# Decoder layer in fp32 split matmuls: other slots and engines for splits and a rounding piece in five of 32 attention units

## The chip, the core and the metric

The kernel runs on one core of one Trainium2 chip. The metric is the device time of one execution in microseconds (us). Most executions of this kernel agree within 0.3%. The core's engines run side by side and wait for each other through semaphores: TensorE (PE) multiplies, VectorE (DVE), ScalarE (ACT) and GpSimd (POOL) work on tiles, SyncE (SP) starts the transfers. PE also has a row of its own for loading weights (PEld).

## The reference

One decoder layer over x of 8 x 256 x 512, with a context of 8 x 256 x 512: rotary causal self-attention with 16 heads of 128, whose weights are a signed exponential; masked cross-attention over the context with 16 heads of 32; a feed-forward part of width 2048 with weights rounded to -1, 0 and 1 and activations rounded to 8 bits. Each of the three is added to x and normalized.

```python
def _L0_attn_ref(...):
    q = jnp.einsum('bpd,hde->bphe', resid_pre, W_Q) + b_Q
    ...
    q = _apply_rotary(q, cos, sin)
    k = _apply_rotary(k, cos, sin)
    scores = jnp.einsum('bqhd,bkhd->bhqk', q, k) / ATTN_SCALE
    ...
    scores = jnp.where(causal[None, None], scores, jnp.zeros((), dtype=scores.dtype))
    max_v = jnp.max(jnp.abs(scores), axis=-1, keepdims=True)
    sgn = jnp.sign(scores)
    attn_w = sgn * jnp.exp(sgn * scores - max_v)
    attn = attn_w / (jnp.sum(jnp.abs(attn_w), axis=-1, keepdims=True) + 1e-06)
    z = jnp.einsum('bkhd,bhqk->bqhd', v, attn)
    out = jnp.einsum('bqhd,hdm->bqm', z, W_O) + b_O
...
def weight_quant(w):
    scale = 1.0 / jnp.clip(jnp.mean(jnp.abs(w)), EPS, None)
    return jnp.clip(jnp.round(w * scale), -1.0, 1.0) / scale
...
x = _layernorm(x + _L0_attn_ref(x, ...), axis=-1)
x = _layernorm(x + _L0_xattn_ref(x, ctx_2048, mask_BxS2_ik0, ...), axis=-1)
x = _layernorm(x + _L0_ffn_ref(x, ...), axis=-1)
```

## The kernel before

**Split products.** A float32 operand is held as two parts, hi (a cast to the matmul type) and lo (the operand minus hi). Each product is three matmuls: hi x hi (L146), hi x lo (L147), lo x hi (L148). So every operand first needs a split: a cast and a subtraction over 128 x 1024 elements. `split` (L155) casts on DVE (L156) and subtracts on a given engine (L157). `half_split` (L181) does one of the two: part 1 is the subtraction (L183), part 0 the cast, on ACT (L185) or on DVE (L187). `x_half` applies it to one half of an x tile, `load_x` loads and splits both halves of one, `load_w` loads and splits a weight.

**Self-attention in 32 units.** A unit is a pair of heads times a pair of batches; the first four units share one head pair. Each takes about 28.1 us. Unit i computes its projections while the attention of unit i-1 runs, and the output projection of unit i-2 its end. A string of letters (`SCHED`, one for unit 0, one for all others) gives the program order, and `emit` walks it. Q is a projection, w and u its evictions on ACT (L308) and DVE (rcos, L314); r and R the rotation on POOL (L318, L324, L326); H and L the split of the rotated tile (L335 on ACT, L342, with the copy L341 of early keys on DVE); V, v, f the values. Of the unit before: s scores (L370, and mm3), a their eviction on ACT (L379, L380), S the causal select on POOL (L385), m the maximum on DVE (L391, L392), x the exponential on ACT (L400), n and N the sum and the normalization on DVE (snorm, L405 and L413, result e), t the transposes on PE (L420), c and k their split, z the product with the values, y and l its split (ACT L447, DVE), o the output projection, d its sum into acc (DVE, L465). The first digit after a letter is the batch half, the second the head.

**Slots.** B0, BA, BV, BW, BX, BY, XA, XB, X0, X1, G0 and G1 in the string are slots that `background(ui)` fills with work for later: loads of the next x and of weights, their splits, and the rounding of feed-forward weights. Units 1 to 3 read x from the input and split it in two halves; later units read the split tile back from DRAM. `wq_round` rounds one chunk of 128 x 1024 in three DVE steps (L219 scale and limit, L221 limit and add, L224 subtract), and then stores it; units 16 to 30 round one chunk each, and unit 17 rounds two (`ROUND`).

**Last unit.** Unit 31 loads the first half of the context (`cr`) and splits it, and loads and splits the second half of the first cross-attention weights (`wk1`); after it follow two value weights (`wv`), the values' bias (in a buffer of the tag aw, which has two), the second context tile (`ctx1`, subtractions on POOL, L157), the projections of keys and values for cross-attention (L146 to L148 into ppj, evicted by L634 and L638), with the attention of the last unit in between them (`tail`).

**Order.** `in_order` fixes the program order on ACT, DVE, POOL and SP up to the end of unit 31, for unit 0 on PE as well. PE's order in units 1 to 31, and every engine's in the stretch after unit 31, are set by the framework's scheduler. Buffers are few (`BUFS`: 5 for weights w, 2 for x tiles xt, 3 for raw loads, 2 for aw; in PSUM, 3 for projections and 1 for scores). The rest of the kernel (cross-attention, feed-forward) goes by a planned order that the change leaves alone.

Of the kernel before, what the change touches and what calls it, by code (L numbers as in the profile page):

```python
# [11 lines left out]
F32R = mybir.dt.float32r  # L12
# [47 lines left out]
SCHED = {  # L60
    "first": (
        "Q000 Q100 Q001 WK w00 u00 Q101 w10 u10 WV r00 R00 BA r10 Q010 Q011 w01 u01 H00 L00 Q110 R10 Q111 w11 u11 H10 L10 r01 V0 v0 V1 v1 "
        "X0 V2 v2 V3 v3 X1 R01 H01 L01 r11 R11 H11 L11 f0 f2 BW"
    ),
    "unit": (
        "B0 BP Q000 s00 Q001 a00 s01 a01 w00 Q010 u00 S0 BA s10 r00 Q011 m0 o00- o01- a10 w01 d00- R00 X0 s11 r01 H00 x0 a11 XA "
        "o10- Q100 S1 Q101 u01 o11- w10 d01- L00 n0 m1 R01 XB r10 H01 N0 u10 R10 L01 x1 Q110 n1 Q111 w11 t00 d11- "
        "t01 V0 v0 BV H10 c01 k01 u11 r11 V1 v1 c00 V2 k00 N1 X1 f0 z00 G0 z01 y0 t10 t11 c10 R11 c11 V3 H11 l0 k10 k11 BX "
        "L10 L11 BY v2 z10 z11 G1 y1 d10- v3 BW f2 l1"
    ),  # L70
# [8 lines left out]
def decoder_kernel(ctx: ExitStack, tc: tile.TileContext, a, out):  # L79
    nc = tc.nc  # L80
# [27 lines left out]
    def T(tag, shape, dt=F32, name=None):  # L108
        return (keep if tag in ("w", "xt") else sb).tile(shape, dt, name=name or tag, tag=tag, bufs=BUFS.get(tag, 1))
# [45 lines left out]
    def split(hi, lo, raw, eng):  # L155
        nc.vector.tensor_copy(hi, raw)  # L156
        eng.tensor_tensor(lo, raw, f32(hi), ALU.subtract)  # L157

    def split_w(raw, tag="w"):
        w = T(tag, [128, 2, 1024], F32R)  # L160
        split(w[:, 0], w[:, 1], raw, nc.vector)
        return w
# [13 lines left out]
    def x_half(t, raw, i, part, eng):  # L176
        tf = t.rearrange("p h k c -> p h (k c)")
        cs = slice(1024 * i, 1024 * i + 1024)
        half_split(tf[:, 0, cs], tf[:, 1, cs], raw, part, eng)

    def half_split(hi, lo, raw, part, eng):  # L181
        if part:
            eng.tensor_tensor(lo, raw, f32(hi), ALU.subtract)  # L183
        elif eng is nc.scalar:
            eng.copy(hi, raw)  # L185
        else:
            eng.tensor_copy(hi, raw)  # L187
# [13 lines left out]
    def wchunk(wi, c):  # L201
        return raw_load(a[f"w{wi + 1}T"][:, 1024 * c : 1024 * c + 1024])

    def wq_abs(raw, wi, c):
        nc.scalar.activation(raw, raw, AF.Abs, accum_out=absum[:, wi, c : c + 1])
# [11 lines left out]
    def wq_round(raw, wi, c, step):  # L217
        if step == 0:
            nc.vector.tensor_scalar(raw, raw, wscale[:, 2 + wi : 3 + wi], 1.0, ALU.mult, ALU.min)  # L219
        elif step == 1:  # L220
            nc.vector.tensor_scalar(raw, raw, -1.0, MAGIC, ALU.max, ALU.add)  # L221
        else:
            q = T("bc", [128, 1024], (BF16, F16)[wi], name="wqt")
            nc.vector.tensor_scalar(q, raw, -MAGIC, None, ALU.add)  # L224
            nc.sync.dma_start(wq_s[wi][:, 1024 * c : 1024 * c + 1024], q)
# [25 lines left out]
    hw, kv0 = {}, {}  # L251
# [233 lines left out]
    units = [Unit(hp, bp) for hp in range(NHP) for bp in range(NBP)]  # L485

    def run(fs):
        for f in fs:
            f()
# [22 lines left out]
    A0, ABS, late = 6, (4, 5, 6, 8, 9, 10, 12, 13), {}  # L512
    ROUND = {16: [0], 17: [1, 2], **{i: [i - 15] for i in range(18, 31)}}

    def background(ui):
        u = units[ui]
        ex = {k: [] for k in ("B0", "BA", "BV", "BW", "BX", "BY", "XA", "XB", "X0", "X1", "G0", "G1", "BP", "WK", "WV")}
        if ui == 0:
            ex["WK"].append(lambda: load_hp(0, "wK", first["wK"]))
            ex["WV"].append(lambda: load_hp(0, "wV", first["wV"]))  # L520
        nx = units[ui + 1] if ui + 1 < len(units) else None
        if nx is not None and nx.hp == 0:
            if ui < 2:
                ex["BA"].append(nx.xload)
            for i, k in enumerate(("X0", "X1") if ui < 2 else ("B0",)):
                ex[k].append(lambda i=i: nx.xsplit(i))
            if ui == 2:
                ex["XA"].append(lambda: x_half(nx.xt, nx.raws[1], 1, 0, nc.scalar))
                ex["XB"].append(lambda: x_half(nx.xt, nx.raws[1], 1, 1, nc.gpsimd))
        elif nx is not None:  # L530
            ex["BA"].append(nx.load)
        if ui == 1:
            ex["BV"].append(units[3].xload)
        if u.hp == 0:
            ex["BA" if ui else "X1"].append(lambda: init_acc(u.bp))
            ex["BA" if ui else "X1"].append(lambda: nc.sync.dma_start(f32(xs[u.bp][:]), f32(u.xt[:])))
        if "wv" in late:
            ex["B0"].append(lambda raw=late.pop("wv"): load_hp(u.hp, "wV", raw["w"]))
        for n, hp, k1 in ([("wO", u.hp, "BW")], [], [("wQ", u.hp + 1, "BW")], [("wK", u.hp + 1, ""), ("wV", u.hp + 1, "")])[u.bp]:
            if (ui or n == "wO") and hp < NHP:  # L540
                raws = {}
                ex["BV" if n == "wV" else "BA"].append(lambda n=n, hp=hp, raws=raws: raws.update(w=raw_load(a[n][hp])))
                if n == "wV":
                    late["wv"] = raws
                elif n == "wK":
                    def hi(raws=raws, hp=hp):
                        w = hw.setdefault(hp, {})["wK"] = T("w", [128, 2, 1024], F32R)
                        half_split(w[:, 0], w[:, 1], raws["w"], 0, nc.scalar)

                    def lo(raws=raws, hp=hp):  # L550
                        w = hw[hp]["wK"]
                        half_split(w[:, 0], w[:, 1], raws["w"], 1, nc.vector)

                    ex["G0"].append(hi)
                    ex["BX"].append(lo)
                else:
                    ex[k1].append(lambda n=n, hp=hp, raws=raws: load_hp(hp, n, raws["w"]))
        if ui in ABS:
            for j in range(2):
                i, rr = 2 * ABS.index(ui) + j, {}  # L560
                ex["BA"].append(lambda i=i, rr=rr: rr.update(w=wchunk(i // 8, i % 8)))
                ex[f"G{j}"].append(lambda i=i, rr=rr: wq_abs(rr["w"], i // 8, i % 8))
        for n, ci in enumerate(ROUND.get(ui, ())):
            cr = {}
            ex["BA"].append(lambda cr=cr, ci=ci: cr.update(w=wchunk(ci // 8, ci % 8)))
            for step, k in enumerate((("G0", "G1", "BW"), ("X0", "X1", "BX"))[n]):
                ex[k].append(lambda step=step, cr=cr, ci=ci: wq_round(cr["w"], ci // 8, ci % 8, step))
        if ui == 1:
            ex["BA"].append(lambda: bo.update(t=bcast("bc", "bO")))
        if ui == len(units) - 2:  # L570
            ex["BA"].append(lambda: kv0.update(wk0r=raw_load(a["wkx"][:, 0:1024])))
            ex["BW"].append(lambda: kv0.update(wk0=split_w(kv0["wk0r"])))
        if ui == len(units) - 1:
            ex["BA"].append(lambda: kv0.update(cr=x_raws(a["ctxT"][0])))

            def ctx_split(i):
                if i == 0:
                    kv0["ctx"] = T("xt", [128, 2, 4, 512], F32R)
                x_split(kv0["ctx"], kv0["cr"][i], i, (nc.vector, nc.gpsimd)[i])

            ex["X0"].append(lambda: ctx_split(0))
            for k, part, e in (("BX", 0, nc.vector), ("BY", 1, nc.gpsimd)):
                ex[k].append(lambda part=part, e=e: x_half(kv0["ctx"], kv0["cr"][1], 1, part, e))
            ex["X0"].append(lambda: kv0.update(wk1r=raw_load(a["wkx"][:, 1024:2048])))
            ex["BW"].append(lambda: kv0.update(wk1=split_w(kv0["wk1r"])))
        if ui == 4:
            ex["BA"].append(setup_late)
        if ui == 5:
            ex["G0"].append(setup_late2)
        if ui in (A0 + 8, A0 + 9):  # L590
            ex["G0"] += [lambda wi=wi: (wq_tot, wq_mean)[ui - A0 - 8](wi) for wi in range(2)]
        if A0 + 2 <= ui < A0 + 18:
            ex["BP"].append(lambda: add_bo(ui - A0 - 2))
        return ex
# [17 lines left out]
    for ui, u in enumerate(units):  # L612
        spec = SCHED["unit" if ui else "first"]
        if ui == 1:
            spec = spec.replace(" V0 v0", "").replace(" t00", " V0 v0 t00")
        emit(spec, u, units[ui - 1] if ui > 0 else None, units[ui - 2] if ui > 1 else None, background(ui))
        if ui == 0:
            in_order(["PE", "Activation", "DVE", "Pool", "SP"])
# [32 lines left out]
    H, steps, tiles, unit, last, readers = {}, [], {}, [None], {}, {}  # L651
# [747 lines left out]
```

## Time and profile before

| what | value |
|---|---|
| median of 3 runs | 1399.37 us |
| lowest, highest | 1399.22, 1401.14 us |
| profiled execution: its time | 1400.85 us |
| profiled execution: its span, first to last instruction | 1399.1 us |
| mean granted TensorE clock | 0.986 |
| unit 0's first matmuls to unit 31's end | 0 to some 915 us |
| DMA traffic | 170.13 MB, mean 122 GB/s |

Times inside a profile count from the first instruction. Busy time of PE contains the time in which it works at a lower granted clock, so a stretch can be full and yet slow. The span in 40 slices of 35 us (each digit the busy share in tenths) shows where the engines are less than full:

```profile
PE   8999999999999999999999999999999999988896
...
PEclk9999999999999999999999999999999999999998
```

### The profile page before, as it was taken

To read this page: it belongs to the slowest core of one execution; us is meant where nothing else is said; L and a number is where in the kernel's file an instruction comes from. 1 tells how busy PE (TensorE), PEld (TensorE's weight loads), DVE (VectorE), ACT (ScalarE), POOL (GpSimd) and SP (SyncE) were. 2 spreads that over 40 slices of the span, in tenths; PEclk is the share of its full clock that TensorE was granted. 3 is DMA by queue.
4 is the path that set the end of the run, shared out by engine and by line. 5 is a ranking of instruction groups with operands and counts; after the bars stand their busy time and mean duration, and the time that the engine had idled before them with its cause. 6 is when DMAs were issued, how large, how long until landed. Compare 5 with 4: busy or idle time off the path is not lost.

```text
span 1399.1 us, 23786 instructions
## 1 busy us (share of the span) xinstructions
PE 1355.8 (97%) x8576; PEld 1085.2 (78%) x8576; DVE 1100.3 (79%) x2040; ACT 876.1 (63%) x1944; POOL 785.7 (56%) x987
## 2 busy tenths in 40 slices
PE   8999999999999999999999999999999999988896
PEld 7789888998899878998899888878667667543342
DVE  7787777778768868887877877968767877798997
ACT  3766776777666656666665666533644445576994
POOL 5666556666665756766665656525033324376763
PEclk9999999999999999999999999999999999999998
DMA  8542342234223234223422442226324424214553
GB/s 280 206 184 107 134 156 106 91 144 161 91 75 121 90 128 162 105 83 126 187 84 98 132 167 98 76 90 197 113 58 126 135 72 140 91 31 91 114 113 98
DMA packets 84903, 170.13 MB, mean 122 GB/s; under 512 B 47025, under 2 KB 57009, under 8 KB 79921
## 3 DMA queue, kind: packets, MB, share of 16 engines
q1 hardware_dynamic: 84784, 168.61, 35.8%
q8 instruction: 68, 1.11, 0.3%
q14 instruction: 51, 0.41, 0.1%
HBM read 130.31 MB, written 27.79 MB: 113 GB/s over the span
## 4 chain that ended last, share of the span: by engine, by line
PE 75%; DVE 14%; issue 3%; POOL 3%; DMA 2%; ACT 2%; SPq 0%; POOLq 0%; DVEq 0%; ACTq 0%
PE ppj L146 12%; PE ppj L147 12%; PE ppj L148 12%; PE pz L146 3%; PE pz L148 3%; PE pz L147 3%; PE pwt L420 3%; PE sc L854 2%; PE den L885 2%; PE psc L370 2%; PE av L869 2%; PE pz L443 2%; PE ppo L146 2%; PE ppo L147 2%; PE ppo L148 2%
## 5 line engine op out<-in xcount | busy, mean ns | idle before, releaser
L318 POOL TENSOR_TENSOR sw<-sw,stab 128x512 f32<-128x512 f32 x128 | 170.5, 1332 | 98.7 <-ACT sw L309 98.2
L146 PE MATMUL ppj<-xt,w 128*128 128x512 f32 x528 | 209.7, 398 | 1.0 <-DVE w L156 0.7
L147 PE MATMUL ppj<-xt,w 128*128 128x512 f32 x528 | 207.2, 392 | 1.1 <-DVE xt L157 1.0
L148 PE MATMUL ppj<-xt,w 128*128 128x512 f32 x528 | 206.7, 392 | 0.0
L146 PE MATMUL ppj<-w,xt 128*128 128x256 f32 (+1 forms) x528 | 157.9, 299 | 1.7 <-DVE u L314 1.7
L148 PE MATMUL ppj<-w,xt 128*128 128x256 f32 (+1 forms) x528 | 152.2, 288 | 0.0
L147 PE MATMUL ppj<-w,xt 128*128 128x256 f32 (+1 forms) x528 | 152.1, 288 | 0.0
L342 POOL TENSOR_TENSOR rh<-u,rh 128x512 fp32r<-128x512 f32 x64 | 97.4, 1522 | 97.1 <-PE ppj L148 85.2
L314 DVE SCALAR_TENSOR_TENSOR u<-ppj,bqk,ctab 128x512 f32<-128x512 f32 x128 | 95.5, 746 | 71.6 <-ACT sw L309 71.1
L308 ACT ACTIVATE sw<-ppj,bqk 64x512 f32<-64x512 f32 x128 | 87.7, 685 | 93.3 <-PE ppj L148 88.4
L326 POOL TENSOR_TENSOR u<-u,sw 128x256 f32<-128x256 f32 (+1 forms) x128 | 131.8, 1029 | 6.4 <-DVE u L314 6.2
L413 DVE SCALAR_TENSOR_TENSOR e<-aw,rd,sg 128x128 f32<-128x128 f32 (+1 forms) x256 | 131.0, 569 | 0.1
L385 POOL TENSOR_SCALAR_AFFINE_SELECT aw<-aw 128x256 f32<-128x256 f32 x128 | 59.2, 486 | 104.5 <-ACT aw L379 104.5
L148 PEld LDWEIGHTS ppj<-xt,w 128*128 128x128 f32 x528 | 99.6, 189 | 21.7 <-DVE w L157 0.3
L400 ACT ACTIVATE aw<-aw,nm 128x256 f32<-128x256 f32 (+1 forms) x256 | 113.3, 444 | 4.9 <-DVE nm L391 2.6
L447 ACT CAST z<-pz 128x512 fp32r<-128x512 f32 x64 | 37.6, 587 | 122.8 <-PE pz L443 122.8
L146 PEld LDWEIGHTS ppj<-xt,w 128*128 128x128 f32 x528 | 99.7, 189 | 18.2 <-DVE w L156 1.0
L147 PEld LDWEIGHTS ppj<-xt,w 128*128 128x128 f32 x528 | 99.6, 189 | 18.3 <-DVE xt L157 1.8
L146 PEld LDWEIGHTS ppj<-w,xt 128*128 128x128 f32 x528 | 102.1, 193 | 3.2 <-issue 1.6
L147 PEld LDWEIGHTS ppj<-w,xt 128*128 128x128 f32 x528 | 102.2, 194 | 0.7
L148 PEld LDWEIGHTS ppj<-w,xt 128*128 128x128 f32 x528 | 101.9, 193 | 0.7
L379 ACT ACTIVATE aw<-psc 128x384 f32<-128x384 f32 x128 | 62.2, 486 | 61.7 <-PE psc L148 59.3
(284 smaller groups left out, 3950.0 us busy)
## 6 DMA issues: line engine op xcount, KB each, us to landing
xt<-xs SPq DMA_DIRECT2D x28, 2048.0 KB, 8.1
xs<-xt SPq DMA_DIRECT2D x4, 2048.0 KB, 13.0
raw<-w1T SPq DMA_DIRECT2D x16, 512.0 KB, 9.6
raw<-w2T SPq DMA_DIRECT2D x16, 512.0 KB, 9.7
raw<-wO SPq DMA_DIRECT2D x8, 512.0 KB, 9.0
acc<-xn SPq DMA_DIRECT2D x4, 1024.0 KB, 8.4
wq<-wqt SPq DMA_DIRECT2D x16, 256.0 KB, 2.4
kx<-ks SPq DMA_DIRECT2D x8, 512.0 KB, 5.0
```

The costliest lines, as they stand in the source:

```text
L146: nc.tensor.matmul(ps, lh, rh, start=first, stop=False)
L147: nc.tensor.matmul(ps, lh, rl, start=False, stop=False)
L148: nc.tensor.matmul(ps, ll, rh, start=False, stop=last)
L308: nc.scalar.activation(sw[0:64], ps[64:128], AF.Identity, bias=bias[64:128])
L314: nc.vector.scalar_tensor_tensor(v3(u), v3(self.ps.pop((h, i))), self.bias(h, i), ctab.to_broadcast([128, 2, 256]), ALU.add, ALU.mult)
L318: nc.gpsimd.tensor_tensor(v3(sw), v3(sw), stab.to_broadcast([128, 2, 256]), ALU.mult)
L326: nc.gpsimd.tensor_tensor(u, u, sw, ALU.add)
L342: (nc.gpsimd if i else nc.vector).tensor_tensor(lo, u if i else u[:, :, 128:256], f32(hi), ALU.subtract)
L379: nc.scalar.activation(aw[:, h], sc3, AF.Abs, scale=1.0 / math.sqrt(DH))
L385: nc.gpsimd.affine_select(aw[:, :, blk], aw[:, :, blk], pattern=[[0, 2], [-1, 128]], compare_op=ALU.is_ge, fill=MASKED, base=0, channel_mu ...
L400: nc.scalar.activation(aw[:, h, blk], aw[:, h, blk], AF.Exp, bias=nm[:, h, i : i + 1], accum_out=rd[:, h, i : i + 1])
L413: nc.vector.scalar_tensor_tensor(e[:, h, blk], aw[:, h, blk], rd[:, h, i : i + 1], sg[:, h, blk], ALU.mult, ALU.mult)
```

## The change

Unit numbers count from 0.

1. Unit 0: of the second half of unit 1's x, the cast goes from DVE to ACT (slot XA, added to the first string behind X0); the subtraction stays on DVE at X1. The load of unit 2's x goes from unit 1's BA to unit 0's BW.
2. Unit 1: the first half of unit 2's x is split at B0 instead of X0; `N0` (normalization of batch half 0) moves ahead of `m1`; the values' projection V0 and its eviction v0 are no longer ahead of t00.
3. Unit 2: the subtraction for the second half of unit 3's x goes from POOL to DVE, and its slot XB to behind N0.
4. Units 17 and 18: unit 17's second rounding chunk is loaded at BV instead of BA, and its three DVE steps, which were at X0, X1 and BX of unit 17, all stand at B0 of unit 18.
5. Unit 31: for the second half of the context, the cast goes from DVE (BX) to ACT (G0), and the subtraction from POOL (BY) to DVE (BW). For wk1, the cast goes from DVE (BW) to ACT (G0); the subtraction stays on DVE at BW.

```diff
     "first": (
-        "X0 V2 v2 V3 v3 X1 R01 H01 L01 r11 R11 H11 L11 f0 f2 BW"
+        "X0 XA V2 v2 V3 v3 X1 R01 H01 L01 r11 R11 H11 L11 f0 f2 BW"
...
     "unit": (
-        "o10- Q100 S1 Q101 u01 o11- w10 d01- L00 n0 m1 R01 XB r10 H01 N0 u10 R10 L01 x1 Q110 n1 Q111 w11 t00 d11- "
+        "o10- Q100 S1 Q101 u01 o11- w10 d01- L00 n0 m1 R01 r10 H01 N0 XB u10 R10 L01 x1 Q110 n1 Q111 w11 t00 d11- "
...
         if nx is not None and nx.hp == 0:
-            if ui < 2:
+            if ui == 0:
                 ex["BA"].append(nx.xload)
-            for i, k in enumerate(("X0", "X1") if ui < 2 else ("B0",)):
-                ex[k].append(lambda i=i: nx.xsplit(i))
-            if ui == 2:
+            ex["X0" if ui == 0 else "B0"].append(lambda: nx.xsplit(0))
+            if ui == 1:
+                ex["X1"].append(lambda: nx.xsplit(1))
+            else:
                 ex["XA"].append(lambda: x_half(nx.xt, nx.raws[1], 1, 0, nc.scalar))
-                ex["XB"].append(lambda: x_half(nx.xt, nx.raws[1], 1, 1, nc.gpsimd))
+                ex["XB" if ui else "X1"].append(lambda: x_half(nx.xt, nx.raws[1], 1, 1, nc.vector))
         elif nx is not None:
             ex["BA"].append(nx.load)
-        if ui == 1:
-            ex["BV"].append(units[3].xload)
+        if ui < 2:
+            ex["BV" if ui else "BW"].append(units[ui + 2].xload)
...
+        if "r2" in late:
+            ex["B0"].append(lambda f=late.pop("r2"): run(f))
         for n, ci in enumerate(ROUND.get(ui, ())):
             cr = {}
-            ex["BA"].append(lambda cr=cr, ci=ci: cr.update(w=wchunk(ci // 8, ci % 8)))
-            for step, k in enumerate((("G0", "G1", "BW"), ("X0", "X1", "BX"))[n]):
-                ex[k].append(lambda step=step, cr=cr, ci=ci: wq_round(cr["w"], ci // 8, ci % 8, step))
+            ex["BV" if n else "BA"].append(lambda cr=cr, ci=ci: cr.update(w=wchunk(ci // 8, ci % 8)))
+            fs = [lambda step=step, cr=cr, ci=ci: wq_round(cr["w"], ci // 8, ci % 8, step) for step in range(3)]
+            if n:
+                late["r2"] = fs
+            else:
+                for k, f in zip(("G0", "G1", "BW"), fs):
+                    ex[k].append(f)
...
-            for k, part, e in (("BX", 0, nc.vector), ("BY", 1, nc.gpsimd)):
-                ex[k].append(lambda part=part, e=e: x_half(kv0["ctx"], kv0["cr"][1], 1, part, e))
             ex["X0"].append(lambda: kv0.update(wk1r=raw_load(a["wkx"][:, 1024:2048])))
-            ex["BW"].append(lambda: kv0.update(wk1=split_w(kv0["wk1r"])))
+
+            def last(part, e):
+                if part == 0:
+                    kv0["wk1"] = T("w", [128, 2, 1024], F32R)
+                x_half(kv0["ctx"], kv0["cr"][1], 1, part, e)
+                half_split(kv0["wk1"][:, 0], kv0["wk1"][:, 1], kv0["wk1r"], part, e)
+
+            ex["G0"].append(lambda: last(0, nc.scalar))
+            ex["BW"].append(lambda: last(1, nc.vector))
...
         if ui == 1:
-            spec = spec.replace(" V0 v0", "").replace(" t00", " V0 v0 t00")
+            spec = spec.replace(" N0 XB", "").replace(" n0 m1", " n0 N0 m1")
```

In unit 1 the strings differ from those of the other units by the last two lines: before, V0 v0 stood ahead of t00; now N0 stands ahead of m1.

## The prediction

> **What bounds the kernel now.** I read the page's busy table first, then the busy time of each engine in stretches of 2 us, and last the timelines of DVE, POOL, ACT and PE around every stretch in which PE is short of 2.00 or its clock under 1.00.
>
> ```profile
> PE 1355.8 (97%) x8576; PEld 1085.2 (78%) x8576; DVE 1100.3 (79%) x2040; ACT 876.1 (63%) x1944; POOL 785.7 (56%) x987
> ```
>
> PE is busy for 97%: only PE's holes can be won. In the stretches (width, then PE, PEld, DVE, ACT, POOL busy with counts, granted clock, DMA share, GB/s) the edited units show these:
>
> ```profile
> 28.00:30.00 2.00, 0.53 (x2) 0.21 (x2) 2.00 (x3) 0.20 (x1) 1.77 (x1) 1.00 0.08 23
> 30.00:32.00 2.00, 2.00 (x7) 1.81 (x8) 1.97 (x3) 1.65 (x5) 1.50 (x2) 0.52 1.03 258
> ...
> 44.00:46.00 2.00, 0.80 (x5) 0.40 (x4) 2.00 (x3) 1.64 (x7) 1.72 (x2) 1.00 1.02 418
> ...
> 82.00:84.00 2.00, 1.49 (x11) 1.24 (x12) 1.97 (x5) 1.44 (x6) 0.10 (x1) 1.00 0.00 0
> ```
>
> ```profile
> 498.00:500.00 2.00, 1.21 (x8) 1.20 (x9) 2.00 (x3) 0.00 (x0) 1.21 (x1) 1.00 0.00 0
> 500.00:502.00 2.00, 1.48 (x8) 1.06 (x7) 1.97 (x5) 0.62 (x1) 1.52 (x2) 1.00 0.00 0
> 502.00:504.00 2.00, 1.01 (x7) 0.80 (x7) 2.00 (x7) 1.80 (x8) 0.00 (x0) 1.00 0.00 0
> ...
> 506.00:508.00 2.00, 2.00 (x11) 2.00 (x11) 0.91 (x3) 1.59 (x6) 2.00 (x3) 0.51 0.03 8
> ```
>
> ```profile
> 910.00:912.00 2.00, 0.81 (x7) 0.56 (x5) 2.00 (x3) 0.00 (x0) 1.55 (x1) 1.00 0.00 0
> 912.00:914.00 2.00, 0.61 (x2) 0.30 (x3) 2.00 (x5) 1.18 (x3) 0.73 (x1) 1.00 0.56 170
> 914.00:916.00 2.00, 2.00 (x5) 1.51 (x6) 2.00 (x3) 0.00 (x0) 0.00 (x0) 0.53 0.23 92
> ```
>
> In each hole DVE is full: PE waits for DVE. After four holes (of 1.6, 1.5, 1.1 and 2.4 us within 3.4 us) the clock stands at 0.50 for about 3.4 us, which costs 1.7 us more each time. Idle and slow clock together: 7.4 us in units 0 and 1 (24 to 52 us), 0.55 in unit 2, 4.9 at 496 to 514, 4.8 at 904 to 932, 17.6 in all. From 84 to 496 and 514 to 904 every stretch that I read is full.
>
> The timelines (start, length, engine and line, [idle before <- releaser]) say why:
>
> ```profile
> 26.44 2.20 DVE L157 TENSOR_TENSOR xt<-raw,xt 128x1024 fp32r<-128x1024 f32 x1
> 28.57 1.56 DVE L341 COPY rf<-u 128x256 f32<-128x256 f32 x2
> ...
> 43.82 2.84 DVE L413 SCALAR_TENSOR_TENSOR e<-aw,rd,sg 128x128 f32<-128x128 f32 x4
> ```
>
> ```profile
> 70.34 5.02 DVE L413 SCALAR_TENSOR_TENSOR e<-aw,rd,sg 128x128 f32<-128x128 f32 x4
> 99.33 1.83 DVE L413 SCALAR_TENSOR_TENSOR e<-aw,rd,sg 128x128 f32<-128x128 f32 x4
> 497.23 0.76 DVE L219 TENSOR_SCALAR raw<-raw,wscale 128x1024 f32<-128x1024 f32 x1 [7.67 <-DMA raw<-w1T]
> ```
>
> The four L413 take 1.83 us without and 5.02 us beside GpSimd's 2.45 us subtraction L183 (70.93): DVE and POOL hold each other up. At 497.23 DVE had waited 7.67 us for a rounding chunk (loaded from 487.21 to 497.13) with all of the unit's attention work queued behind it.
>
> **Units 0 and 1 (edits 1 and 2).** In unit 0 one cast (1.12 us, 25.29) leaves DVE; ACT takes it at 1.08 us (the seven L185 copies) in ACT's idle 2.29 us before 22.93: hidden, and at most 1.08 late if the cover goes. The DVE subtraction moves from 26.44 to 25.86 and, about 1.1 us long when POOL is not in its way, no longer ends at 28.64. POOL's L318 and L326 (1.74 and 2.13) still stand ahead of the second key copy, so the first scores move from 29.98 to about 28.3, while the second wait for POOL's L342 as before: 31.45 against 31.87. In unit 1 unit 2's first half goes to the unit's start, where DVE idles 3.58 us before 36.53; the first rcos then comes 1.0 earlier, and snorm of half 0, moved ahead of m1, starts at 41.45 instead of 43.82. Behind it on DVE m1 waits, and ACT's exps for m1: but x1's start is held by ACT and POOL at 44.9 against 45.0, so the second snorm ends at 52.85 against 54.32, and unit 2's first matmul comes at 54.3 against 55.48. That is 1.2; I take 0.9, since a slow phase may stay. Bounds: -0.5 (m1 behind snorm passes its loss on) to 2.4 (one slow phase of 1.7 gone too). The load moved from unit 1 to unit 0's end keeps its place in SP's queue: nothing.
>
> **Unit 2 (edit 3).** The subtraction goes from POOL to DVE behind snorm. L413 falls from 5.02 to 1.83 (3.2 off), the subtraction adds 1.22 (L183 on DVE, its mean): 2 us less before the next DVE step. That removes 0.04 + 0.51 of PE idle at 80 to 84: 0.55; bounds 0.3 to 0.55.
>
> **Units 17 and 18 (edit 4).** Chunk 2's load moves to a later slot, in the same SP order; its three DVE steps (L219, L221, L224) go to unit 18's start. The load landed at 497.1, unit 18 starts near 512: 15 us margin. There they cost 0.7 + 0.7 + 0.7 to 0.9, about 2.1 us, hidden by the wait for the first projections: the 2.25 us split at unit 2's start left DVE still 1.40 idle before rcos (63.42). Without that cover 0.95 would come back. What falls away is the whole hole: idle 0.42 + 0.79 + 0.52 + 0.99 + 0.25 + 0.08 + 0.10 = 3.15, and 1.72 of slow clock: 4.87. Bounds 3.9 to 4.9.
>
> **Last unit (edit 5).** Before: ctx's second half on DVE (1.2) and POOL (2.56 at 908.99), and the key weights' cast and subtraction on DVE after it, hold proj at 911 to 914: idle 0.31 + 1.88 + 0.70, slow clock 1.7, and 0.5 at 930.
>
> ```profile
> 904.84 0.58 ACT L447 CAST z<-pz 128x512 fp32r<-128x512 f32 x1 [2.90 <-PE pz L443]
> 922.54 2.40 POOL L157 TENSOR_TENSOR xt<-raw,xt 128x1024 fp32r<-128x1024 f32 x1
> 930.82 0.49 PE L370 MATMUL psc<-rf 128*128 128x128 f32 x2 [0.49 <-ACT sg L380]
> ```
>
> After: two ACT copies, 2 x 1.08 = 2.16, fit the 2.90 idle before 904.84; PE runs on. But the program order of the tail, which the scheduler sets, changes too: on POOL both subtractions of ctx1 (L157, 2.40 each) now stand before the last unit's select L385, and both casts before nm on DVE; before, one stood behind it. Chain: DVE's last subtraction ends 912.05 and frees the buffers; the wv1 load goes out at 912.1, the two of ctx1 at 913.25 and 913.7; by the landings before (3.6, 3.8, 5.2 us) they are there at 915.7, 917.2, 918.7. DVE's cast ends 918.7, POOL's first subtraction 921.1, second 924.2, select 925.0 (first select before: about 922), nm 925.95, exps 927.75, sum and e 929.65; e frees the second aw buffer (the other holds the values' bias), a10 then ends 930.6, and the unit's last scores start at 930.65: 930.82 before. So the path gains 0.2, while PE, through with its other work at 926.3, idles 4.35 us there. Then a slow phase follows, as after every hole of 1.1 or more: 1.9 (1.1 to 2.8, by where its 3.4 us fall). Net -1.7; bounds -2.6 to +4.3.
>
> **Sum.** 0.9 + 0.55 + 4.87 - 1.7 = 4.6. The profiled execution's span is 1399.1, its time 1400.85, 1.5 above the median; I take the difference off the median: 1399.37 - 4.6 = 1394.8. Bounds' sum for the likeliest case: 1392.5 to 1397.
>
> **Rivals.** A: no hole in the tail, because the select does not have to wait (loads 2 to 4 us earlier, or POOL's two subtractions at 1.2, as DVE's are). For it: PE has other work until 926.3, so only 4.35 must go; against: POOL's L157 took 2.40 twice. Then edit 5 gives up to +4.3: 1399.37 - 10.6 = 1388.8.
> B, slower: the three tail loads, now issued together, land as late as the w1T one (9.92) instead of 3.6 to 5.2. For it: that size is the same 512 KB; against: DMA is nearly free there (share 0.23 to 0.88 before). 6 us more on the chain: edit 5 -7.7, total +1.4: 1400.8, with a second slow phase 1402.5. It decides from when the scores restart later than about 935.
> C: edit 4 is idle because DVE waits at unit 18's start as long as it did in 17. Against: 15 us of margin; for: DVE is full from 508 to 518. Gain without it: -0.2: 1399.6.
> D: the clock does not fall in the tail after the 4.35 us. Against: it fell after 1.1. Then edit 5 is +0.2, total 6.5: 1392.9. [...]
>
> **How the numbers follow.** Forecast 0.45, A 0.14, B 0.16, C 0.10, D 0.06, unseen 0.09. A change of 0.2%, 2.8 us, is about what a measurement of this kernel tells from none. Under 1396.6: nearly all of the forecast (0.43), A, D, 0.05 of the unseen: 0.68. Over 1402.2: half of B and 0.04: 0.12. Between: 0.20. The range 1390 to 1400.5 leaves out two thirds of A and half of B, about 0.2.
>
> **What would show it.** L185 copies on ACT ten, POOL's L183 gone. L413 at 70 us near 1.8. All stretches of 496 to 514 at 2.00 with clock 1.00, and three L219 to L224 steps at the start of unit 18. Stretches of 24 to 52 us fuller by about 1. In the last unit a PE idle of some 4 us before scores released by ACT sg, with two L157 of POOL before its L385, and a clock near 0.5 behind. Wrong it is if PE idles anew where snorm was moved, or if the tail's loads take 9 us.

## The result and the profile after

| | before | changed |
|---|---|---|
| median of 6 runs | 1400.45 us | 1389.93 us |
| lowest, highest | 1399.22, 1401.14 | 1389.21, 1391.52 |
| profiled execution: time, span | 1400.85, 1399.1 | 1391.33, 1389.6 |

The ratio is 0.9928, with a 95% interval of 0.9916 to 0.9941: 10.1 us less (8.3 to 11.8); the two medians are 10.5 apart. The prediction said 4.6 less. The 1389.93 lies 0.07 below the low end of its range (1390 to 1400.5), which was made from a median of 1399.37.

The page's busy table of the changed kernel:

```profile
PE 1348.5 (97%) x8564; PEld 1081.6 (78%) x8576; DVE 1094.3 (79%) x2039; ACT 879.1 (63%) x1947; POOL 782.5 (56%) x985
```

The 2 us stretches that answer to those shown of before (width, PE, PEld, DVE, ACT, POOL busy, clock, DMA share, GB/s):

```profile
28.00:30.00 2.00, 0.89 (x3) 0.19 (x1) 1.97 (x2) 0.00 (x0) 1.92 (x2) 1.00 0.70 236
...
32.00:34.00 2.00, 0.74 (x7) 0.74 (x7) 1.97 (x2) 1.21 (x4) 2.00 (x2) 1.00 0.96 283
...
44.00:46.00 2.00, 0.90 (x4) 0.34 (x3) 2.00 (x3) 1.43 (x3) 2.00 (x3) 1.00 0.96 395
46.00:48.00 2.00, 0.97 (x8) 0.98 (x9) 2.00 (x4) 0.63 (x4) 0.69 (x1) 1.00 0.56 234
48.00:50.00 2.00, 2.00 (x12) 2.00 (x11) 1.31 (x3) 1.98 (x7) 1.30 (x2) 0.51 0.22 86
...
498.00:500.00 2.00, 2.00 (x13) 1.67 (x13) 1.05 (x4) 1.71 (x7) 1.92 (x4) 1.00 0.00 0
...
506.00:508.00 2.00, 2.00 (x19) 2.00 (x18) 2.00 (x5) 1.74 (x6) 0.18 (x1) 1.00 0.01 4
...
920.00:922.00 2.00, 1.04 (x5) 0.54 (x3) 1.96 (x6) 0.60 (x2) 0.00 (x0) 1.00 0.35 131
922.00:924.00 2.00, 1.36 (x8) 1.25 (x9) 0.20 (x1) 1.65 (x5) 0.00 (x0) 1.00 0.02 4
```

Three things are to be seen. The hole around unit 17 is gone altogether. In units 0 and 1 there are as many holes as before, at other places (28 to 30, 32 to 34, 44 to 48), and one slow clock instead of two. In the tail a smaller hole stands at 921 to 923, and no slow clock follows it.

A better scale than such sums is the cast of z on ACT (L447): it comes twice for each unit's attention, 64 times in all, in the same order in both kernels. Where the distance between two casts shrinks, time was won:

| z cast | before | changed | ahead by | won since the row above |
|---|---|---|---|---|
| 3rd (attention of unit 1, in unit 2) | 81.89 | 83.55 | -1.66 | -1.66 |
| 4th (the same, second half) | 86.18 | 86.82 | -0.64 | 1.02 |
| 32nd (in unit 16) | 480.27 | 480.91 | -0.64 | 0.00 |
| 35th (in unit 18) | 539.48 | 533.87 | 5.61 | 6.25 |
| 61st (in unit 31) | 904.84 | 899.27 | 5.57 | -0.04 |
| 64th (end of the tail) | 947.73 | 939.56 | 8.17 | 2.60 |
| end of the span | 1399.1 | 1389.6 | 9.5 | 1.3 |

So edit 4 brings 6.25, edit 5 2.6, edit 3 1.02; the first two units lose 1.66, and 1.3 comes from the stage after, which the change does not touch. The first and the last of these rows are partly chance, as the experiments show.

### The profile page after: what moved, and what is told of

Read it like the earlier page. It is cut to its first block, busy times and chain, and to the rows that moved or that the text cites. A ratio compares the mean times of both kernels' runs of the same rounds, so it can differ in the third digit from the quotient of the medians.

```text
span 1389.6 us, 23773 instructions
## 1 busy us (share of the span) xinstructions
PE 1348.5 (97%) x8564; PEld 1081.6 (78%) x8576; DVE 1094.3 (79%) x2039; ACT 879.1 (63%) x1947; POOL 782.5 (56%) x985
## 4 chain that ended last, share of the span: by engine, by line
PE 81%; DVE 11%; POOL 3%; issue 2%; ACT 2%; DMA 1%; SPq 0%; POOLq 0%; DVEq 0%; ACTq 0%
PE ppj L146 12%; PE ppj L147 12%; PE ppj L148 12%; PE pz L146 3%; PE pz L148 3%; PE pz L147 3%; PE pwt L420 3%; PE sc L867 2%; PE den L898 2%; PE av L882 2%; PE ppo L146 2%; PE ppo L147 2%; PE ppo L148 2%; PE psc L370 2%; PE pz L443 2%
## 5 line engine op out<-in xcount | busy, mean ns | idle before, releaser
L146 PE MATMUL ppj<-xt,w 128*128 128x512 f32 x528 | 209.0, 396 | 0.3 <-DVE w L156 0.3
L146 PE MATMUL ppj<-w,xt 128*128 128x256 f32 (+1 forms) x528 | 157.1, 298 | 0.0
L314 DVE SCALAR_TENSOR_TENSOR u<-ppj,bqk,ctab 128x512 f32<-128x512 f32 x128 | 95.5, 747 | 67.7 <-ACT sw L309 67.2
L413 DVE SCALAR_TENSOR_TENSOR e<-aw,rd,sg 128x128 f32<-128x128 f32 (+1 forms) x256 | 127.2, 554 | 0.1
L400 ACT ACTIVATE aw<-aw,nm 128x256 f32<-128x256 f32 (+1 forms) x256 | 113.3, 444 | 6.1 <-DVE nm L391 6.0
L447 ACT CAST z<-pz 128x512 fp32r<-128x512 f32 x64 | 37.6, 587 | 120.4 <-PE pz L443 120.4
L146 PEld LDWEIGHTS ppj<-xt,w 128*128 128x128 f32 x528 | 99.4, 188 | 17.0 <-DVE w L156 0.8
L146 PEld LDWEIGHTS ppj<-w,xt 128*128 128x128 f32 x528 | 101.6, 192 | 0.6
```

The source lines that it names most:

```text
L146: nc.tensor.matmul(ps, lh, rh, start=first, stop=False)
L314: nc.vector.scalar_tensor_tensor(v3(u), v3(self.ps.pop((h, i))), self.bias(h, i), ctab.to_broadcast([128, 2, 256]), ALU.add, ALU.mult)
L400: nc.scalar.activation(aw[:, h, blk], aw[:, h, blk], AF.Exp, bias=nm[:, h, i : i + 1], accum_out=rd[:, h, i : i + 1])
L413: nc.vector.scalar_tensor_tensor(e[:, h, blk], aw[:, h, blk], rd[:, h, i : i + 1], sg[:, h, blk], ALU.mult, ALU.mult)
```

## The experiments

Each kernel was timed in five rounds (4 to 11 runs) beside the kernel before on the same chip. The diffs show only the parts of lines that change, and ... stands for what is left out. The time of one kernel scatters: 42 runs of the kernel before in the three sets go from 1397.59 to 1403.91. So the times tell about 1.5 us, and a distance inside a profile, which repeats within 0.1 where nothing chances, tells the rest. In the table, A is the start of unit 0's first matmul of the values (L146, ppj<-w,xt), and the casts are those of z; a slow phase is a stretch of some 3.4 us at clock 0.50.

| profile | edits | key weights cast | A | A to 3rd cast | slow phase near 30, near 47 | 32nd to 35th | 61st to 64th | 64th to end |
|---|---|---|---|---|---|---|---|---|
| before | none | 11.27 | 18.41 | 63.48 | yes, yes | 59.21 | 42.89 | 451.34 |
| e_unit2 | 3 | 10.94 | 18.24 | 62.23 | no, yes | 59.09 | 41.31 | 451.11 |
| e_unit17 | 4 | 11.16 | 18.27 | 62.02 | no, yes | 52.95 | 42.91 | 451.40 |
| e_last | 5 | 12.32 | 19.45 | 63.55 | yes, yes | 59.08 | 40.24 | 450.02 |
| e_no01 | 3, 4, 5 | 12.18 | 19.34 | 62.11 | no, no | 52.95 | 40.25 | 450.03 |
| f_no01ctx | 3, 4, 5, DVE | 12.07 | 19.20 | 62.06 | no, no | 52.95 | 38.35 | 449.60 |
| f_edit1ctx | 1, 3, 4, 5, DVE | 12.49 | 20.67 | 61.50 | no, no | 52.95 | 38.33 | 450.34 |
| e_noN0 | all but 2's order | 12.10 | 19.23 | 62.81 | no, yes | 52.95 | 40.25 | 448.93 |
| changed | all | 12.51 | 20.61 | 62.94 | no, yes | 52.96 | 40.29 | 449.99 |
| f_after | all | 11.74 | 18.86 | 63.47 | no, yes | 52.95 | 40.24 | 450.18 |
| e_wkfirst | all | 11.18 | 18.72 | 63.73 | no, yes | 52.96 | 40.29 | 449.53 |
| e_ctxdve | all, DVE | 11.66 | 18.81 | 63.39 | no, no | 52.95 | 38.41 | 450.16 |
| f_ctxdve | all, DVE | 11.36 | 18.73 | 63.62 | no, yes | 52.95 | 38.35 | 450.74 |
| e_units01 | 1, 2 | 12.51 | 22.34 | 62.39 | no, yes | 59.06 | 42.91 | 449.20 |

("DVE": the second context tile's subtractions on DVE. In e_units01 a slow phase also came at 16.5; its A is 1.7 later than that of the changed kernel, whose key weights were cast at the same time. Its phase near 47 is two in a row.)

### Each edit alone

**e_units01**: edits 1 and 2 of the diff, with unit 2's subtraction left on GpSimd.

```diff
-ex["XB" if ui else "X1"].append(lambda: x_half(nx.xt, nx.raws[1], 1, 1, nc.vector))
+ex["XB" if ui else "X1"].append(lambda: x_half(nx.xt, nx.raws[1], 1, 1, nc.vector if ui == 0 else nc.gpsimd))
```

(That is against the changed kernel; edits 3, 4 and 5 are left out.)

> Edits 1 and 2 alone (units 0 and 1), all else as before. Theory S (the start is chance): the 2.2 us by which unit 0 ran late in the profile after (key weights cast at 12.51 instead of 11.27, their subtraction 2.19 instead of 1.23 us) belongs to that execution, not to the change; then in this profile the key weights are cast near 11.3, one slow phase of 1.7 us is gone, and the first unit that runs at full pace is 0.5 to 1.5 us earlier than before: 0.5 to 1.5 us faster. Rival O (the order costs): snorm ahead of m1 holds up m1, the exps and the second snorm, whatever the start: last snorm of the unit later than 53.0 (51.46 before), and the time 0.5 to 1.7 us longer than before.

Measured: 1400.17 (before 1400.50), ratio 1.000 (0.9991 to 1.0010): no gain to be seen, though the interval (1.3 less to 1.4 more) still holds the 0.9 that was forecast. Its key weights were again cast at 12.51, so this run alone does not tell whether the late start is chance; the table does: kernels with unit 0 as before had it at 10.94 to 12.32, kernels with the changed unit 0 at 11.36 to 12.51 (e_wkfirst, which loads them in another order, aside). A late landing comes with and without the change. The rival's place was right: the second snorm starts 16.47 us behind unit 1's first rcos, 14.93 before (its 54.45 also contains the late start). Its price, 0.5 to 1.7 us, the time neither shows nor wholly rules out.

**e_unit2**: edit 3.

```diff
-"R01 XB r10 H01 N0 u10"
+"R01 r10 H01 N0 XB u10"
-x_half(nx.xt, nx.raws[1], 1, 1, nc.gpsimd)
+x_half(nx.xt, nx.raws[1], 1, 1, nc.vector)
```

> Edit 3 alone (unit 2: subtraction on DVE behind snorm). By the prediction's term the four L413 near 70 us fall from 5.02 to about 1.8 and the time by 0.55 us; by the distance between the landmarks in the two profiles (the z cast of unit 2's two halves) the gain is 1.0. The rival that DVE loses as much as POOL gives back: 0.

Measured: 1397.45 (before 1400.50), ratio 0.9983 (0.9974 to 0.9992): 2.4 less (1.1 to 3.6). The four L413 fell to 1.83, and the 3rd and 4th casts stand 3.26 apart (4.29 before): 1.03, as the landmarks said. The time's interval begins just above that. This profile also has a slow phase less in unit 0 and in the tail; whether that makes up the rest of the 2.4 in the other runs is not shown. DVE in unit 2 of this kernel, the subtraction being the L183 behind:

```profile
68.91 1.83 DVE L413 SCALAR_TENSOR_TENSOR e<-aw,rd,sg 128x128 f32<-128x128 f32 x4
70.66 1.21 DVE L183 TENSOR_TENSOR xt<-raw,xt 128x1024 fp32r<-128x1024 f32 x1
```

**e_unit17**: edit 4.

```diff
-ex["BA"].append(lambda ...: cr.update(w=wchunk(ci // 8, ci % 8)))
+ex["BV" if n else "BA"].append(lambda ...: cr.update(w=wchunk(ci // 8, ci % 8)))
...
+if "r2" in late:
+    ex["B0"].append(lambda f=late.pop("r2"): run(f))
```

> Edit 4 alone (units 17 and 18). Theory R: a hole costs PE its idle time, the slow clock, and a refill at every restart (a first matmul shows 0.4 to 0.5 us instead of a spacing of 0.23); by the pace between the z casts (28.1 us a unit; 33.9 and 28.55 here) the holes cost 6.2 to 6.3: 6.2 us faster. Rival I: only idle and slow clock count, 4.87 us faster, and the rest that the profile after shows comes from other edits that met there.

Measured: 1393.33 (before 1400.50), ratio 0.9959 (0.9946 to 0.9971): 5.7 less (4.1 to 7.6), and from the 32nd to the 35th cast 6.26 less. The time alone does not tell 6.2 from 4.87, since both lie in its interval; the distance does. The z casts on ACT, first of before, then of this kernel (start, length, ..., [ACT's idle before]):

```profile
480.27 0.59 ACT L447 CAST z<-pz 128x512 fp32r<-128x512 f32 x1 [1.27 <-PE pz L443]
510.93 0.59 ACT L447 CAST z<-pz 128x512 fp32r<-128x512 f32 x1 [3.09 <-PE pz L443]
...
539.48 0.59 ACT L447 CAST z<-pz 128x512 fp32r<-128x512 f32 x1 [3.14 <-PE pz L443]
```

```profile
478.69 0.59 ACT L447 CAST z<-pz 128x512 fp32r<-128x512 f32 x1 [1.26 <-PE pz L443]
503.54 0.59 ACT L447 CAST z<-pz 128x512 fp32r<-128x512 f32 x1 [3.14 <-PE pz L443]
...
531.64 0.59 ACT L447 CAST z<-pz 128x512 fp32r<-128x512 f32 x1 [3.14 <-PE pz L443]
```

From 480.27 to 510.93 are 30.66, from 478.69 to 503.54 only 24.85, the step of nearly every other unit (24.85 to 24.92, one of 25.29). But theory R was not right in how it makes up the 6.2. Before and e_last had a slow phase at 504 and 506, e_unit2 and e_units01 had none there, and the distances are 59.21, 59.08 and 59.09, 59.06. So the slow clock cost 0.15 at most, not 1.7. What it does is seen in the stretch of 8 us behind it, before and then e_units01 at the same place of the program:

```profile
508.00:516.00 8.00, 7.81 (x57) 6.85 (x56) 8.00 (x17) 2.64 (x7) 3.96 (x4) 1.00 0.01 4
```

```profile
510.70:518.70 8.00, 6.87 (x45) 5.63 (x45) 8.00 (x17) 2.77 (x8) 3.87 (x4) 1.00 0.02 8
```

DVE is busy for all of the 8.00 in both. With the slow clock PE is busy for 7.81, without it 6.87: at full clock PE gets its work done sooner, and then waits for the same DVE. DVE, which had lost 7.67 us to the load, sets the pace there, and neither PE's idle nor its clock is the price.

**e_last**: edit 5.

```diff
-for k, part, e in (("BX", 0, nc.vector), ("BY", 1, nc.gpsimd)):
...
+ex["G0"].append(lambda: last(0, nc.scalar))
+ex["BW"].append(lambda: last(1, nc.vector))
```

> Edit 5 alone (last unit). The prediction's term: 1.7 us slower, with a PE idle of 4.35 before the last scores and a slow clock behind it. By the profile after: the context's loads go out as soon as the raw buffers of the value weights are read, two us earlier than the prediction had it, so the select ends near 923 on this kernel's clock, PE idles 1.6 there without a slow phase, and the time is 2.6 us shorter. Rival A of the prediction (no hole at all): 4.3 shorter.

Measured: 1395.91 (before 1400.50), ratio 0.9974 (0.9963 to 0.9985): 3.6 less (2.1 to 5.2). From the 61st to the 64th cast 40.24: 2.65 less than before, e_unit17 and e_units01 (42.9, a slow phase at 907 to 918 in each), 1.07 less than e_unit2, which has no slow phase there (41.31). Here a slow phase did cost 1.6 (three profiles with one, one without). Edit 5 takes away the hole at 911 to 914 and leaves a later one of 1.60 us, which no phase followed.

### Parts taken back

**e_no01**: the changed kernel with units 0 and 1 as before.

```diff
-X0 XA V2 v2
+X0 V2 v2
...
-spec.replace(" N0 XB", "").replace(" n0 m1", " n0 N0 m1")
+spec.replace(" V0 v0", "").replace(" t00", " V0 v0 t00")
```

> The changed kernel with edits 1 and 2 taken back (units 0 and 1 as before). Theory Z: the two edits give nothing that is left after unit 2, the whole gain is edits 3, 4 and 5: 1.0 + 6.2 + 2.6 = 9.8 below before, as the changed kernel (10.1 by its ratio). Theory P (the prediction's term holds, and only a late landing of the key weights hid it): 0.9 slower than the changed kernel, so 9.2 below before. Theory L (the two edits lose): 0.5 to 1.5 faster than the changed kernel, 10.6 to 11.6 below before.

Measured: 1390.64 (before 1401.01), ratio 0.9925 (0.9911 to 0.9938): in the median, theory Z; but its five runs go from 1386.98 to 1391.38, and its interval holds what Z, P and L expect. The profile is on the side of L: A to the 3rd cast 62.11, 62.94 to 63.73 with all edits.

**e_noN0**: only unit 1's order taken back.

```diff
-spec.replace(" N0 XB", "").replace(" n0 m1", " n0 N0 m1")
+spec.replace(" V0 v0", "").replace(" t00", " V0 v0 t00")
```

> The changed kernel with unit 1's program order as before (snorm behind m1, values ahead of the first transposes), while edit 1 and unit 2's x at the unit's start stay. Theory O (snorm ahead of m1 costs what the rest of edits 1 and 2 gains: m1 came at 46.90 instead of 42.86): the second snorm of the unit starts 1 to 2 us earlier against the first scores than in the changed kernel, and the time is 0.5 to 1.5 us shorter. Rival: the order does not matter, because POOL and ACT hold the second half: equal within 0.3.

Measured: 1389.04 (before 1401.01), ratio 0.9919 (0.9905 to 0.9932). From unit 1's first rcos to the 3rd cast the profile has 45.84; the changed kernel 46.50, f_after 46.50, e_ctxdve 46.52; kernels without edits 1 and 2 45.34 to 45.40. So the order costs 0.7 and the rest of the moves 0.5. The second snorm starts 22.21 us behind the first scores, 23.35 in the changed profile: 1.1 earlier. That is theory O, at the low end of its range. Its time agrees (0.9919, 0.9928 for the changed kernel), but the intervals overlap.

**e_wkfirst**: the changed kernel, key weights loaded ahead of the tables.

```diff
-setup_consts()
 for n in ("wK", "wV"):
     first[n] = T("z", [128, 1024])
     nc.sync.dma_start(first[n], a[n][0])
+    if n == "wK":
+        setup_consts()
```

> The changed kernel with the key weights' first load issued ahead of the three small loads of tables and biases. Theory D (the late start is the landing of the key weights, 10.9 to 12.5 us in six profiles): the cast of the key weights comes at 11.0 or earlier, PE does not wait for it, and the first projections of values come 0.5 to 2.2 us earlier than in the changed profile; the time 0.3 to 1.5 shorter. Rival (DMA bandwidth holds everything to the same end): the tables then land late instead, rcos (L314) waits for them, and nothing is gained.

Measured: 1390.10 (before 1401.01), ratio 0.9926 (0.9914 to 0.9939): nothing gained. The key weights were cast at 11.18 without a wait for the load, and A came at 18.72, as in f_after (18.86), whose weights landed late; the first scores at 28.88 and 28.80. A late landing of half a microsecond does not reach the first scores; with the weights cast at 12.51, in the changed profile, they came at 30.02. The first rcos came at 13.61 in e_wkfirst and f_after alike, so the rival's reason, late tables, is not seen either.

### The tail, and the best of the parts

**e_ctxdve** and, beside the changed kernel, **f_ctxdve**:

```diff
-ctx1 = load_x(a["ctxT"][1], nc.gpsimd)
+ctx1 = load_x(a["ctxT"][1], nc.vector)
```

> The changed kernel with the two subtractions of the second context tile on DVE instead of POOL, so that POOL's select of the last unit no longer stands behind them. Theory T (the select's place makes the remaining hole of 1.6 us before the last scores): select near 913 to 914 on the changed profile's clock instead of 917, no PE idle over 0.5 before the last scores, and 1.6 to 1.9 us faster than the changed kernel. Rival: DVE, then with 2.4 us more between the casts and nm, delays nm as much: hole the same within 0.5, time equal.

Measured: 1388.57 (before 1401.01), ratio 0.9916 (0.9902 to 0.9929); 61st to 64th cast 38.41, 1.9 less than with the subtractions on POOL: theory T. The changed kernel's POOL and PE in the tail, then f_ctxdve's POOL and DVE:

```profile
911.61 2.40 POOL L157 TENSOR_TENSOR xt<-raw,xt 128x1024 fp32r<-128x1024 f32 x1 [4.75 <-DVE xt L156]
914.64 2.39 POOL L157 TENSOR_TENSOR xt<-raw,xt 128x1024 fp32r<-128x1024 f32 x1 [0.63 <-DVE xt L156]
916.99 0.76 POOL L385 TENSOR_SCALAR_AFFINE_SELECT aw<-aw 128x256 f32<-128x256 f32 x2
...
922.64 0.49 PE L370 MATMUL psc<-rf 128*128 128x128 f32 x2 [1.60 <-ACT sg L380]
```

```profile
911.71 1.22 POOL L385 TENSOR_SCALAR_AFFINE_SELECT aw<-aw 128x256 f32<-128x256 f32 x2 [6.01 <-ACT aw L379]
...
912.58 0.40 DVE L391 TENSOR_REDUCE nm<-aw 128x2 f32<-128x256 f32 x1
912.91 1.21 DVE L157 TENSOR_TENSOR xt<-raw,xt 128x1024 fp32r<-128x1024 f32 x1
```

In the changed kernel POOL's two subtractions end at 916.99, only then comes the select, and the last scores start at 922.64 after 1.60 of idle. With the subtractions on DVE the select comes at 911.71 (912.9 on the changed profile's clock, whose 61st cast is 1.15 later), the maximum (L391) at 912.58, and no wait of PE is left before the scores.

> The changed kernel once more, as the measure for the three beside it. Its profile again: z casts 31 to 34 at 52.96 us, last unit 40.3 us from its first z cast to the tail's last; slow clock phases in units 0 and 1 none, one or two by chance. Time 9.5 to 11 below before.

Measured: 1390.14 (before 1400.47), ratio 0.9923 (0.9910 to 0.9936), as the first time; one slow phase, near 47.

> The changed kernel with the second context tile's subtractions on DVE, again, beside the changed kernel. Theory T: 1.9 us shorter from the last unit's first z cast to the tail's last (38.4 instead of 40.3), and 1.5 to 2.3 us in the time. Rival: given back in the later stage: equal within 0.5.

Measured: 1389.17, ratio 0.9917 (0.9902 to 0.9931): 1.0 less than f_after, less than expected; the profile has the 1.9 in the tail (38.35) and 0.6 more in the stage after (450.74 against 450.18), which scatters. The time alone would not have settled it.

**f_no01ctx** (as f_ctxdve, edits 1 and 2 taken back as in e_no01) and **f_edit1ctx** (as f_ctxdve, edit 2 taken back). The diff is that of f_edit1ctx:

```diff
-ex["X0" if ui == 0 else "B0"].append(lambda: nx.xsplit(0))
+ex["X0" if ui < 2 else "B0"].append(lambda: nx.xsplit(0))
...
-spec.replace(" N0 XB", "").replace(" n0 m1", " n0 N0 m1")
+spec.replace(" V0 v0", "").replace(" t00", " V0 v0 t00")
```

> As f_ctxdve, with edits 1 and 2 taken back. Theory L (the two edits lose 1.2 us from the second unit's first rcos on, 1.1 of it by snorm ahead of m1 and the split at the unit's start where only 2.1 us and not 3.6 are idle when no slow clock phase comes; they gain the phase of 1.4 us only in the executions that have one near 30 us): 0.3 to 1.2 us faster than f_ctxdve. Theory P (the prediction's term): 0.9 slower. Theory Z: equal within 0.3.

Measured: 1388.51, ratio 0.9907 (0.9893 to 0.9920): 0.7 less than f_ctxdve in the median, as theory L had it, though the intervals overlap; A to the 3rd cast 62.06 against 63.62, 1.56 less, of which 0.5 is lost again by a start that was later there.

> As f_ctxdve, with edit 2 taken back and edit 1 kept (the cast of unit 1's x on ACT; unit 2's x split at X0 and X1, snorm behind m1). Theory L: the first rcos of unit 1 comes at most 0.6 earlier against the start of the value projections than with edit 1 taken back, because ACT's first scores' eviction waits for POOL's rotation in both; equal to f_no01ctx within 0.5, and no slower than f_ctxdve. Rival (edit 1 alone is what helps): 0.8 or more faster than f_no01ctx.

Measured: 1387.57 (1385.82 to 1388.48), ratio 0.9900 (0.9886 to 0.9915): the fastest kernel of all, 2.6 below the changed kernel beside it. A to the 3rd cast is 61.50, the shortest of the fourteen; the first rcos comes 15.91 behind A, 0.75 earlier than in f_no01ctx, somewhat more than theory L allowed. Its median is 0.94 below that of f_no01ctx, as the rival had it (0.8 or more), though the intervals overlap. In the profiles its 4th cast comes later (85.44, 84.51 in f_no01ctx). Whether edit 1 alone helps is not settled: its A was the late 20.67, and a late A is partly made up by the wait behind it.

DVE in unit 1 shows what edit 2 does. Before, then f_no01ctx, f_after (with ACT's first exponential of x1, L400) and f_edit1ctx (rcos L314, maximum L391, snorm L413):

```profile
36.53 0.75 DVE L314 SCALAR_TENSOR_TENSOR u<-ppj,bqk,ctab 128x512 f32<-128x512 f32 x1 [3.58 <-ACT sw L309]
...
42.86 0.42 DVE L391 TENSOR_REDUCE nm<-aw 128x2 f32<-128x256 f32 x1 [0.27 <-POOL aw L385]
```

```profile
35.86 0.75 DVE L314 SCALAR_TENSOR_TENSOR u<-ppj,bqk,ctab 128x512 f32<-128x512 f32 x1 [2.14 <-ACT sw L309]
```

```profile
35.83 0.74 DVE L314 SCALAR_TENSOR_TENSOR u<-ppj,bqk,ctab 128x512 f32<-128x512 f32 x1
...
41.98 3.76 DVE L413 SCALAR_TENSOR_TENSOR e<-aw,rd,sg 128x128 f32<-128x128 f32 x4
45.66 0.41 DVE L391 TENSOR_REDUCE nm<-aw 128x2 f32<-128x256 f32 x1
...
46.10 0.40 ACT L400 ACTIVATE aw<-aw,nm 128x128 f32<-128x128 f32 x1 [1.26 <-DVE nm L391]
```

```profile
42.92 0.42 DVE L391 TENSOR_REDUCE nm<-aw 128x2 f32<-128x256 f32 x1 [0.27 <-POOL aw L385]
```

The 3.58 us of DVE idle before rcos, in which the prediction hid a split, belong to an execution with a slow phase at 30; without one they are 2.14, and the split takes 2.9 (cast and subtraction at 34.23 and 35.49 in the changed profile). And with snorm ahead, the maximum m1 comes at 45.66 instead of 42.9; ACT waits 1.26 us for it before its exps, and the second snorm comes later with them.

## Why the prediction was right or wrong

The direction was right, the size was not. Beside the forecast, the profiled executions miss by -2.6 in units 0 and 1 (partly chance), +0.5 in unit 2, +1.4 in units 17 and 18, +4.3 in the last unit, and +1.3 in a stage that was not forecast. That the time lies so near the range at all is owed to the part of rival A in it.

**Units 0 and 1: +0.9 forecast; no gain seen.** The times do not tell 0.9 from nothing: 0 with the two edits alone, 0.7 lost between f_no01ctx and f_ctxdve, 0.5 won between e_no01 and e_wkfirst (which has all edits), all with overlapping intervals. The profiles do: from the first rcos to the 3rd cast 46.50 to 46.52 with all edits, 45.34 to 45.40 without edits 1 and 2, a loss of 1.1. The step that failed is "m1 waits, and ACT's exps for m1: but x1's start is held by ACT and POOL at 44.9". x1 started at 46.0 to 47.3 in the five profiles of the whole change and its tail variants (48.25 in e_units01), held by DVE's m1, because the snorm ahead of m1 takes 3.8 us beside POOL (3.77 from 43.20 in the changed profile, with POOL at work up to 46.69; 1.83 from 99.33 in the profile of before, where POOL is idle from 99.95 on). The cover "DVE idles 3.58 us" was 2.14. The term's lower bound, -0.5, was set for just this, and was too small by the profiles. The first scores did come earlier (at 28.8 in f_after, 28.3 forecast), and nothing was gained by it: the second stand 3.2 behind, since ACT evicts the first only after a cast that waits for POOL's rotation. The phase near 30 came in two of six profiles with the old order and cost 1.4 there; it came in none of the eight with the changed unit 0, which so few profiles do not tell from chance.

**Unit 2: +0.55 forecast, 1.02 measured.** The mechanism was right (L413 1.83, L183 1.21). Mis-sized was the term: the 0.04 + 0.51 of PE idle shown there is about half of what the unit lost.

**Units 17 and 18: 4.87 forecast, 6.1 to 6.25 measured.** Mechanism and cover were right: in the changed profile the three steps stand in unit 18 at 505.81, 508.61 and 510.90, and PE stays at 2.00, although they take 3.8 us and not 2.1. Mis-sized was the sum of 3.15 idle and 1.72 of slow clock, whose second part cost 0.15 at most. Without the slow phase idle rises to 4.0 in nine holes. Some of the last 2 us is hidden in "busy", since each matmul is counted for some 0.16 us longer than the spacing of two (0.39 and 0.23): nine times that is 1.4, an estimate, and the rest stays open. The distance of two casts would have given the right number before the fact.

**Last unit: -1.7 forecast, +2.6 measured.** The place was right: POOL's subtractions ahead of the select, PE idle before the last scores released by ACT's sign. Two sizes were off. The hole was 1.60, not 4.35. The step that failed is "DVE's last subtraction ends 912.05 and frees the buffers; the wv1 load goes out at 912.1": it goes out when the first value weights' split is done (902.07 on DVE). SyncE's issues in the changed profile:

```profile
902.09 0.33 SPq L152 DMA_DIRECT2D raw<-wvx  x1
906.32 2.02 SPq L152 DMA_DIRECT2D raw<-ctxT  x2
```

That is 902.09, 4.4 us before the prediction's place on this time scale (912.1 less the 5.6 won before). So the value weights were split before the context landed, DVE's cast came 1.7 earlier, and the last scores 2.4. And no slow phase followed the hole in any of the six profiles that have it. The 1.9 set for it is the price of an event that did not come.

**The rest, 1.3, was not forecast.** From the 64th cast to the end the unchanged code takes 448.9 to 451.4 in fourteen profiles: 451.1 to 451.4 in three of the four with the old last unit (449.20 in the fourth), 448.9 to 450.7 in the ten with the new one. So it scatters, and a part may belong to edit 5; that is not settled.

**The rivals.** A's time, 1388.8, was nearest, by luck: its condition, no hole in the tail, held only in f_ctxdve and its like, and edit 4 and the last stage brought what the tail did not. B and C did not come: the context landed within some 4 us of its issue (median 4.1 in the changed profile), and edit 4 gave all that the stall had cost. D was right that the clock would not fall in the tail, but behind a hole of 1.60 us and not of the 4.35 for which it was said. What 4.35 us of idle would have brought there, no run shows; in the profile of before the clock did fall to 0.50 (1265.70 to 1272.52) in and behind PE's wait of 6.83 us that ends at 1267.42.

## What to carry to other kernels

Price a hole by the distance between the same two instructions in a disturbed and an undisturbed unit, not by PE's idle plus slow clock: in unit 17 the idle of 3.15 us was about half of the 6.1 to 6.25 that the hole cost, and the slow clock cost 0.15 at most there, where DVE set the pace. An idle time that is to hide moved work has to be there in executions without a chance event (here it was 3.58 us with one, 2.14 without); ask what made it. Where an engine's order changes, look at what now stands behind the moved instruction (here the maximum behind snorm, the select behind two subtractions): these cost 0.7 us and 1.9 us, and were seen in the program order before any run.

## What the runs showed of the hardware

Up to the end of the tail the profile of before has four slow clock phases, which begin at 30.08, 47.14, 504.53 and 914.13 us. Each is 3.41 us long, at clock 0.50, and in the 3.41 us ahead of it PE idles for 1.60, 1.33, 1.60 and 2.58 us. The changed profile has one, at 48.03, with 1.91 us of PE idle in the 3.41 us ahead of it. The 1.60 us of idle before 922.64 in its tail are as much as before 30.08 and 504.53, and yet the clock stays at 1.00 in the 3.41 us behind them. Idle is counted between modelled ends of matmuls, so these sums are rough. Whether a hole brings a phase also changes from execution to execution: the hole at 911 to 914 did so in three of four profiles with the old last unit, the hole of unit 17 in two of four, the 1.60 us hole of the changed tail in none of six. What decides it, these runs do not show.

What a phase costs differs from place to place: 1.6 us in the last unit (42.89 to 42.91 from the 61st to the 64th cast with one, 41.31 without), 1.4 near 30 us (63.48 and 63.55 from A to the 3rd cast with one, 62.02 and 62.23 without), 0.2 or less near 47 us (62.02 and 62.23 with one, 62.06 and 62.11 without), and 0.15 or less in unit 17 (59.08 and 59.21 from the 32nd to the 35th cast with one, 59.06 and 59.09 without), where DVE sets the pace behind it. And the first key weights' load, issued alike in all but one of the kernels, was cast between 10.94 and 12.51 us.
